# Layer 1 of a four-layer graph network on one Trainium2 core: its last eighth of sources in two pieces, one of them multiplied inside layer 0's last groups

## The chip, the core and the metric

The kernel runs on one core of one Trainium2 chip. The metric is the device time of one execution in microseconds (us); the kernel before has a median of 7455.67 us over 8 runs (7449.52 to 7474.21). The engines are named as the profile names them: PE (TensorE, with PEld for its weight loads), DVE (VectorE), ACT (ScalarE), POOL (GpSimd) and SP (SyncE, whose queue issues most DMAs here).

## What is computed

8192 nodes with 32 features, 262144 edges sorted by destination. Four message-passing layers, each followed by a residual sum and a layer norm over the 32 features:

```python
x = _layernorm(x + _L0_gnn_ref(x, L0_gnn_weight, src, dst, edge_type_64), axis=-1)
x = _layernorm(x + _L1_gnn_ref(x, edge_index, edge_weight), axis=-1)
x = _layernorm(x + _L2_gnn_ref(x, edge_index), axis=-1)
x = _layernorm(x + _L3_gnn_ref(x, edge_index, edge_attr_4, edge_attr_32, ...), axis=-1)
```

Layer 0 sums, at each destination, the source's row times one of 64 matrices. Layer 1 sums `x[src] * w` (w the edge's weight) and layer 2 sums `x[src]`. Layer 3 is an edge network and is not touched here.

## The kernel before, in words

The 8192 nodes stand as 64 blocks of 128 (a block's nodes on the 128 partitions). `LC = 8` blocks make a piece of 1024 nodes, and there are `NQ1 = 8` pieces.

**Layer 0** is a loop over 256 groups g of 1024 edges. For each group POOL gathers the eight sets of 128 rows by indirect DMA (L454), twelve groups ahead (`AHEAD`). The first four gathers of group g+12 wait for group g's own matmuls (`sums_of[g]`), the other four for what PE has been given by then (`now(PE)`). DVE builds one-hot rows (L583) and splits the gathered rows into three bf16 parts (L858 to L863). PE multiplies (eight matmuls, L897). Every fourth group DVE takes the sums out (`bank_out`, L869). As soon as all edges of a piece have passed, `windows` (L575) adds the shifted sums in PSUM and `normalize` (L525 to L537) writes the piece of `x_b`, layer 1's input. Piece k is known from group `ready(k)` on; the last piece, 7, only after group 255.

**Counts as dense matrices.** Groups 8 to 207 also make layer 1's weights and layer 2's counts as dense matrices: `matrices(i)`, 256 times, one-hot products on PE (L654), evicted by ACT (L658 for the counts, L659 for the weights into `st_a`) and stored by SP (L664 `famat`, L666 `fcmat`). A *square* `(c, z)` is the weights of 1024 sources (piece z) to 256 destinations (column c, 32 of them): 1 MB in `famat`, loaded by SP (L695) into a slot of 2048 words on each partition (`slot1`; three slots serve layer 0, three more the part behind it).

**Layer 1** is the sum over all 32 x 8 squares. `products(n, ...)` (L717) multiplies one square: 8 matmuls of a 128x32 block of `x_b` with 256 columns, four of them side by side in four column strips of the array (in the profile each fp32 matmul stands as two records, so a square is 16). The result, four strips by 256 columns, is taken to SBUF by ACT (`take`, L726), turned back and added over the strips by PE (`turn_back`, L736, two matmuls with `stack` as the moving operand), and added to `y1` by DVE (`add_up`, L752).

A planner written out by hand, `plan()`, decides which squares layer 0's groups multiply while their engines have time: `RATE` squares a group fall due (3.0 from group 200 on), a job is a run of pieces of one column, and at most two jobs end in one group, because bank 6 has two halves as accumulators (`bank[:, 6, 256*h:...]`) and `sums1` two. The order on PE within a group is: the group's eight L897 matmuls, `turn_back()` of the jobs that ended a group earlier, `matrices`, then `layer1(g)` with this group's squares. The squares wait for `acc_free`, which is the last `add_up` on DVE. Each square's slot is loaded again by `pump()` when PE has marked the square before it as used.

In this plan squares of piece 5 run in groups 198 to 218, squares of piece 6 (32 of them) in groups 230 to 245, two a group. From group 246 to 255 no group has a square. Piece 7 is normalized after group 255, and its 32 squares are left over (`late`).

**The tail** multiplies these 32 squares, one column a step: `products` (L717), `take` of 128x256 (L726), and, one step behind, `turn` (L980, two matmuls) into an output bank; every fourth step a whole piece is normalized for layer 2's input (with the three bf16 parts, L542 to L546). Six squares' loads are ahead of PE. Layer 2 (L1033) follows when the last piece is normalized.

Of the kernel before, what the change touches and what calls it, by code (L numbers as in the profile page):

```python
# [68 lines left out]

RATE = lambda g: 1.5 if g < 200 else 3.0  # L70


def plan():

    normed, n = [], 0
    for g in range(GG):
        if g >= 2 and (g - 2) % 4 == 3:
            while n < NQ1 and ready(n) <= g - 1:
# [24 lines left out]
    if job is not None:  # L103
        out[-1][4] = True
    return out
# [45 lines left out]
AW = 41200  # L151
NQ1 = 8
WIN = 48
# [8 lines left out]
def in_order(ctx: ExitStack, tc, x, a, w0, w1, b1, w2, si, keep):  # L162
# [11 lines left out]
    for k in range(2):  # L174
        m[f"amat{k}"] = dram.tile([NC1 // 2, NQ1, P * 2048 + 2304], FP, name=f"famat{k}")
    m["cmat"] = dram.tile([CB, P, 2048], U8, name="fcmat")
# [27 lines left out]
def raw_layers(tc, x, a, w0, w1, b1, w2, si, m, bad):  # L204
# [7 lines left out]
    ytab, xtab, hist, cmat = (m[k] for k in ("ytab", "xtab", "hist", "cmat"))  # L212
    amat = [m["amat0"], m["amat1"]]

# [42 lines left out]
    assert cut.at == 16384  # L257
    st_a = cut(2, 8, 4 * 64).rearrange("p b z (q h w) -> p b z q h w", q=4, h=2)
    st_c = cut(2, 4, 2, 256, dt=U8)
# [254 lines left out]

    lnf, lns = m["lnf"], m["lns"]
    x_st = Landing(tc, "st_x")
    ln_last = [None]

    def normalize(l, c, acc, pm, x_in, x_out, x3=None, more=None):


        ds = slice(c * LC, (c + 1) * LC)
        y, yc, sq = (lnf[:, k].rearrange("p (d f) -> p d f", f=D) for k in range(3))
        V.after(pm, ln_last[0])
# [4 lines left out]
        own(V, V.e.tensor_scalar(lns[:, 1], lns[:, 0], 1.0 / D, None, op0=OP.mult))  # L529
        vm = V.mark(V.e.tensor_sub(yc, y, lns[:, 1, :, None].to_broadcast([P, LC, D])))  # L530
        A.after(vm)
# [4 lines left out]
        xo = x_out[:, ds, :]  # L536
        ln_last[0] = V.mark(V.e.tensor_tensor(xo, yc, lns[:, 3, :, None].to_broadcast([P, LC, D]), op=OP.mult))  # L537
        if x3 is not None:
# [12 lines left out]

    def windows(c, acc, free):

        d0 = c * LC
        todo = []
        for j in [0, 1, 2, 3, -2, -1, 4]:
            lo, hi = 0, LC
# [73 lines left out]
    def matrices(i):  # L631
# [14 lines left out]
        for q in range(4):  # L646
# [4 lines left out]
            for j in range(4):  # L651
                for h in range(2):
# [11 lines left out]
        st_ld[b].add(S.e.dma_start(amat[i // 128][i // 8 % 16, :, 0:P * 2048].rearrange("z (p w) -> p z w", w=2048)[:, :, 256 * (i % 8):256 * (i % 8 + 1)],  # L664
                                   st_a[:, b].rearrange("p z q h w -> p z (q h w)")))
        stored[i] = st_ld[b].add(S.e.dma_start(cmat[i], st_c[:, b].rearrange("p u h c -> p (u h c)")))  # L666
# [6 lines left out]
    items = [(o[1], o[2]) for o in order1] + late  # L673
    m_ld = [Landing(tc, f"ld_m{k}") for k in range(8)]
    land1, used1, loaded = {}, {}, [0]
    acc_free = [None]
    sums1_free = [None, None]
    turned = []
    added = []
    normed = {}  # L680

    def slot_of(n):

        r = n - n_in
        if r < 0:
            return 3 + n % 3, n - 3
        order = [0, 1] + [3 + (n_in + k) % 3 for k in range(3)] + [2]
        return order[r % 6], n - 6 if r >= 6 else n - 5 if 2 <= r < 5 else None

    def load1(n, *more):  # L690

        c, z = items[n]
        k, before = slot_of(n)
        S.after(stored[8 * c + 6], stored[8 * c + 7], used1.get(before), *more)
        land1[n] = m_ld[k].add(S.e.dma_start(slot1[k], amat[c // 16][c % 16, z, 0:P * 2048].rearrange("(p w) -> p w", w=2048)))  # L695

    def pump():

        while loaded[0] < n_in + 5:
            n = loaded[0]  # L700
            c, z = items[n]
            before = slot_of(n)[1]
            if made < 8 * (c + 1) or (before is not None and before >= 0 and before not in used1):
                break
# [4 lines left out]
    def products(n, acc, first, last):  # L709

        c, z = items[n]
        k = slot_of(n)[0]
        PE.after(land1[n], normed[z])
        mv = slot1[k].rearrange("p (u h s j) -> p s u h j", h=2, s=8, j=4)
        for s in range(8):
            q = s % 4
            ins = PE.e.matmul(acc[q * D:(q + 1) * D, :].rearrange("p (u h j) -> p u h j", h=2, j=4),  # L717
                              x_b[:, 8 * z + s, :], mv[:, s], start=(first and s < 4), stop=(last and s >= 4),
                              tile_position=(0, q * D))
# [9 lines left out]
    def turn_back():  # L729
# [4 lines left out]
        for c, h, k, am in todo:  # L734
            for d in range(2):
                ins = PE.e.matmul(bank[:, 6, 256 * h + d * D:256 * h + (d + 1) * D], sums1[:, k, d * P:(d + 1) * P], stack,  # L736
                                  start=True, stop=True)
# [7 lines left out]
    def add_up():  # L745
# [3 lines left out]
        while added:  # L749
            c, h = added.pop(0)  # L750
            o, v = y1[:, 2 * c:2 * c + 2, :], bank[:, 6, 256 * h:256 * h + 2 * D].rearrange("p (d f) -> p d f", f=D)
            acc_free[0] = own(V, V.e.tensor_copy(o, v) if c not in begun1 else V.e.tensor_add(o, v, o))  # L752
            begun1.add(c)
# [3 lines left out]
    def layer1(g):  # L757

        ended = []
        while order1 and order1[0][0] == g:  # L760
            _, c, z, first, last, h = order1.pop(0)
            n = n_in - len(order1) - 1
            PE.after(acc_free[0])
            pm = products(n, bank[:, 6, 256 * h:256 * (h + 1)], first, last)
            pump()
            if last:
                ended.append((c, h))
        for c, h in ended:
            turned.append((c, h, h, take(sums1[:, h], bank[:, 6, 256 * h:256 * (h + 1)], pm, sums1_free[h])))
        pump()  # L770
# [34 lines left out]
    def early_counts(g):  # L805

        k = g - soon[0]
        if k == 0:
            ring_free[0] = ring_free[1] = now(PE)
            for n in (n_in, n_in + 1):  # L810
                load1(n, stored[CB - 2], stored[CB - 1])
# [118 lines left out]
    for c in range(NC1):  # L930
        if c not in begun1:
            V.e.memset(y1[:, 2 * c:2 * c + 2, :], 0.0)
    while loaded[0] < min(len(items), n_in + 6):
        load1(loaded[0], *end)
# [37 lines left out]
    def turn(l, c, n, am):  # L972

        nb = 2 if l == 1 else 4
        kk = 128 if l == 1 else 96
# [7 lines left out]
        if d0 + nb == LC:  # L983
            out_free[o] = normalize(l, c * nb // LC, bank[:, 2 + o, 0:LC * D], pm, x_b if l == 1 else x_a,
                                    x_a if l == 1 else x_b, x3 if l == 1 else None,
# [6 lines left out]
    n = n_in  # L992
    for c in range(NC1):
        b = c % 2
        PE.after(sum_bank[b])
        for e in range(got[c], NQ1):
            pm = products(n, bank[:, b, 0:256], e == got[c], e == NQ1 - 1)
            if n + 6 < len(items):
                load1(n + 6)
            n += 1  # L1000
        sum_bank[b] = am = take(sums[:, b, 0:256], bank[:, b, 0:256], pm, sum_free[b])
        if pend:
            turn(*pend)
        pend = (1, c, c, am)
        if c == 0:
            widen(0, [2])
# [193 lines left out]
    for q in range(NQ + LAG3 + 2):  # L1200
# [73 lines left out]
        if 0 <= c < NQ and c % 2 == 1:  # L1274
# [9 lines left out]
            while done < NB // LC and ready(done) <= g + 1:  # L1284
                k, wp = w_bank()
                acc = bank[:, 3 + 2 * k, 0:LC * D]
                windows(done, acc, (w_free[k], gm))
                w_free[k] = normalize(3, done, acc, PE.mark(written(3 + 2 * k, 256)), z, x_a)
                done += 1
# [471 lines left out]
```

## Time and profile before

| | |
|---|---|
| median of 8 runs | 7455.67 us |
| the profiled execution's own time | 7456.69 us |
| its span | 7455.0 us |
| PE busy | 5089.0 us (68%) |
| DVE busy | 4413.7 us (59%) |
| POOL busy | 4141.1 us (56%) |
| ACT busy | 2252.3 us (30%) |
| layer 0's last eight matmuls (L897, group 255) start | 4002.56 us |
| first product of the tail (L717) | 4013.60 us |
| first matmul of layer 2 (L1033) | 4110.82 us |

Times are counted from the span's start. A line of the timeline is: start, duration, engine, line of the kernel, operation, what it writes and reads, shape, how many records are merged in it, and in brackets how long the engine had been idle and what ended that ("remote" when the profile finds no releaser). A line of the windows view gives the length of a stretch, each engine's busy time with its number of instructions, the granted TensorE clock, the DMA engines' share and GB/s. Starts of matmuls are recorded; their ends are modelled, so what tells when PE had really finished is the start of the instruction that waited for it.

### The profile page before, as it was taken

To read this page: it belongs to the slowest core of one execution; us is meant where nothing else is said; L and a number is where in the kernel's file an instruction comes from. 1 tells how busy PE (TensorE), PEld (TensorE's weight loads), DVE (VectorE), ACT (ScalarE), POOL (GpSimd) and SP (SyncE) were. 2 spreads that over 40 slices of the span, in tenths; PEclk is the share of its full clock that TensorE was granted. 3 is DMA by queue.
4 is the path that set the end of the run, shared out by engine and by line. 5 is a ranking of instruction groups with operands and counts; after the bars stand their busy time and mean duration, and the time that the engine had idled before them with its cause. 6 is when DMAs were issued, how large, how long until landed. Compare 5 with 4: busy or idle time off the path is not lost.

```text
span 7455.0 us, 89563 instructions
## 1 busy us (share of the span) xinstructions
PE 5089.0 (68%) x34750; PEld 3360.6 (45%) x34750; DVE 4413.7 (59%) x9506; ACT 2252.3 (30%) x3323; POOL 4141.1 (56%) x4236
## 2 busy tenths in 40 slices
PE   7236566656666666667337977787878787877777
PEld 3125555555555555555224534444444444444444
DVE  3246566566565565555324647666666676676666
ACT  5223333333333333333101832222222222222222
POOL 3655555454454444444661666666666666666664
PEclk7556776777777777777555989888989888888889
DMA  9324444545655656667536731111111111111111
GB/s 352 92 56 142 132 144 141 171 143 165 207 163 188 207 182 205 215 216 247 183 119 229 274 92 25 24 25 21 25 24 24 25 24 25 24 25 24 24 24 18
DMA packets 583331, 865.52 MB, mean 116 GB/s; under 512 B 102640, under 2 KB 441840, under 8 KB 549360
## 3 DMA queue, kind: packets, MB, share of 16 engines
q1 hardware_dynamic: 448320, 782.88, 30.3%
q0 software_dynamic: 134144, 73.67, 6.5%
q8 instruction: 276, 4.52, 0.3%
q10 hardware_dynamic: 432, 3.15, 0.1%
q14 instruction: 159, 1.30, 0.1%
HBM read 454.48 MB, written 404.88 MB: 115 GB/s over the span
## 4 chain that ended last, share of the span: by engine, by line
PE 37%; another core or an unknown queue 25%; DVE 20%; ACT 9%; issue 7%; DMA 2%; POOL 1%; SPq 0%; DVEq 0%; ACTq 0%; POOLq 0%
PE bank L654 14%; PE bank L1221 7%; DVE f_arena L1256 4%; PE bank L1211 4%; ACT f_arena L659 3%; ACT f_arena L658 3%; PE bank L1033 3%; DVE f_arena L1252 3%; PE bank L717 2%; DVE f_arena L588 2%; DVE f_arena L1249 2%; DVE f_arena L1240 1%; ACT bank L1190 1%; PE bank L475 1%
## 5 line engine op out<-in xcount | busy, mean ns | idle before, releaser
L454 POOL DMA_INDIRECT f_arena<-fytab,f_row x2048 | 1961.6, 958 | 1795.6 <-PE bank L654 745.9
L454 POOL DMA_INDIRECT f_arena<-fxtab,f_src x2048 | 1942.2, 948 | 1108.7 <-issue 564.9
L654 PE MATMUL bank<-f_arena 64*128 64x128 f32 x16384 | 1517.7, 353 | 933.9 <-ACT f_arena L659 522.1
L654 PEld LDWEIGHTS bank<-f_arena 64*128 64x128 f32 x16384 | 1385.3, 257 | 1042.2 <-issue 549.0
L1221 PE MATMUL bank<-f_arena 128*128 128x344 f32 x4096 | 1484.8, 506 | 54.6 <-issue 54.4
L658 ACT ACTIVATE f_arena<-bank 128x512 uint8<-128x512 f32 x1024 | 612.8, 598 | 1787.2 <-remote 859.3
L1221 PEld LDWEIGHTS bank<-f_arena 128*128 128x128 f32 x4096 | 815.9, 210 | 630.8 <-issue 368.0
L1211 PE MATMUL bank<-f_arena 64*128 64x256 f32 x4096 | 662.9, 447 | 549.6 <-ACT bank L1190 436.9
L1190 ACT ACTIVATE bank<-f_arena 128x1024 f32<-128x1024 f32 x512 | 526.2, 1029 | 1141.9 <-DVE f_arena L1256 681.0
L1211 PEld LDWEIGHTS bank<-f_arena 64*128 64x128 f32 x4096 | 393.2, 207 | 940.6 <-ACT bank L1190 563.2
L1249 DVE TENSOR_TENSOR f_arena<-bank,f_arena 128x256 f32<-128x256 f32 x512 | 214.0, 418 | 872.5 <-remote 536.2
L638 DVE TENSOR_TENSOR f_arena<-bank,f_arena 128x1024 f32<-128x1024 bf16 x256 | 312.8, 1222 | 647.0 <-PE bank L654 423.3
L659 ACT ACTIVATE f_arena<-bank 128x512 f32<-128x512 f32 x1024 | 611.0, 597 | 0.0
L640 DVE TENSOR_TENSOR f_arena<-bank,f_arena 128x2048 f32<-128x2048 bf16 x256 | 586.6, 2291 | 8.8
L1256 DVE TENSOR_TENSOR f_arena<-bank,f_arena 128x256 f32<-128x256 f32 x1536 | 550.3, 413 | 0.0
L1177 ACT ACTIVATE f_arena<-bank,f_arena 128x512 f32<-128x512 f32 x256 | 175.7, 686 | 1122.8 <-remote 649.9
L717 PE MATMUL bank<-f_arena,f_x_b 128*32 128x256 f32 x4096 | 394.5, 525 | 63.5 <-DMA f_arena<-famat 21.2
L897 PE MATMUL bank<-f_arena 128*128 128x96 bf16 x2048 | 181.3, 238 | 260.5 <-DVE f_arena L863 135.1
L588 DVE TENSOR_TENSOR f_arena<-bank,f_rel 128x512 f32<-128x512 f32 x512 | 348.3, 680 | 0.0
L1252 DVE TENSOR_TENSOR f_arena<-bank,f_arena 128x512 f32<-128x512 f32 x512 | 348.2, 680 | 0.0
L643 DVE TENSOR_TENSOR f_arena<-f_arena,bank 128x1024 f32<-128x1024 f32 x256 | 309.6, 1209 | 0.0
L752 DVE TENSOR_TENSOR f_arena<-bank,f_arena 128x64 f32<-128x64 f32 x127 | 28.5, 224 | 470.2 <-PE bank L736 364.8
(149 smaller groups left out, 4651.1 us busy)
## 6 DMA issues: line engine op xcount, KB each, us to landing
famat<-f_arena SPq DMA_DIRECT2D x256, 1024.0 KB
f_arena<-famat SPq DMA_DIRECT2D x256, 1024.0 KB, 5.3
fytab<-f_arena SPq DMA_DIRECT2D x64, 1024.0 KB
fcmat<-f_arena SPq DMA_DIRECT2D x256, 256.0 KB
f_arena<-fcmat SPq DMA_DIRECT2D x16, 4096.0 KB, 14.8
f_arena<-fytab,f_row POOLq DMA_INDIRECT x2048
f_arena<-fxtab,f_src POOLq DMA_INDIRECT x2048
f_arena<-laid_ea SPq DMA_DIRECT2D x64, 512.0 KB
```

The costliest lines, as they stand in the source:

```text
L454: return G.e.indirect_dma_start(out=dest, out_offset=None, in_=table, in_offset=bass.IndirectOffsetOnAxis(ap=ix, axis=0))
L588: return V.e.tensor_tensor(o, iota[:, None, :].to_broadcast([P, n, P]), rel[:, t:t + n, None].to_broadcast([P, n, P]), op=OP.is_equal)
L640: V.e.tensor_tensor(oh_l[:, b], iota2[:, None, :, 0].to_broadcast([P, 16, P]), meta_l[:, pp, k0:k0 + 16, None].to_broadcast([P, 16, P]), o ...
L654: ins = PE.e.matmul(two[:, h].rearrange("p (c s j) -> p c s j", s=64, j=4)[:, :, :, j], oh_l[hs_, b, 4 * q + j, :], oh_k[hs_, b, 4 * q + j ...
L658: A.e.activation(st_c[:, b, q], two[:, :, 0:256], AF.Copy)
L659: pair_free[u] = am = A.mark(A.e.activation(st_a[:, b, :, q].rearrange("p z h w -> p h z w"), two[:, :, 256:512].rearrange("p h (z w) -> p ...
L717: ins = PE.e.matmul(acc[q * D:(q + 1) * D, :].rearrange("p (u h j) -> p u h j", h=2, j=4), x_b[:, 8 * z + s, :], mv[:, s], start=(first an ...
L1190: return A.mark(A.e.activation(wp, b2_s[:, None, :].to_broadcast([P, 4, 256]), AF.Copy))
L1211: ins = PE.e.matmul(wp[:, t, :], hs[hp, q // 2 % 2, c0:c0 + P], w2_s[hp], start=False, stop=True, skip_group_check=True)
L1221: ins = PE.e.matmul(bank[:, g % 2, 0:MW], oh[:, c % NO, t, :], p[:, c % NP, t, :], start=(c % 2 == 0 and t == 0), stop=(c % 2 == 1 and t = ...
L1252: V.e.tensor_tensor(pq[:, :, 0:128].rearrange("p t (o k) -> p t o k", k=16), wp[:, :, 0:128].rearrange("p t (o k) -> p t o k", k=16), a0[: ...
L1256: ins = V.e.tensor_tensor(pq[:, :, 128 + 64 * mm:192 + 64 * mm].rearrange("p t (o i) -> p t o i", i=8), wp[:, :, 192:256].rearrange("p t ( ...
```

## The change

The pieces are written down as a list `SEG`: seven of 8 blocks, and two of 4 blocks (blocks 56 to 59 and 60 to 63). `NQ1` becomes 9. `known(z)` takes the place of `ready` for layer 0: piece 7 (4 blocks) is known at group 241 and normalized at group 245; piece 8 is normalized after group 255.

- The weights of the last eighth get an array of their own, `flast`, 32 columns x 2 pieces of 512 KB; `matrices` stores each matrix's share in it with one more DMA (256 more in all), and ACT's eviction writes runs of 16 words where it wrote 32.
- Half a slot (1024 words) is now the unit: twelve halves, of which six are layer 0's ring; a full square takes two, a half square one. The order of the words within a square changes with it, and so does the access pattern of the moving operand.
- From group 210 on up to four jobs may end in a group (`ROOMS`); the accumulators 2 and 3 are the halves of bank 2, which `matrices` no longer needs then, and `sum1` has four.
- The plan that comes out: groups up to 209 as before; piece 5 ends in group 216 (groups 210, 213, 214 and 215 have three squares where they had two); piece 6 takes groups 230 to 240 with three squares each (the last two); groups 246 to 253 have the 32 half squares of piece 7, four each, four jobs each.
- The tail has 32 half squares (512 sources, four matmuls each). Two columns share a bank and make one step: `take` is 128x512, `turn` has four matmuls, and there are 16 steps. Twelve half loads are ahead of PE.
- `windows` and `normalize` work on a piece of any number of blocks.

```diff
+SEG = [(8 * k, 8) for k in range(7)] + [(56, 4), (60, 4)]
+NQ1 = len(SEG)
+ROOMS = lambda g: 4 if g >= 210 else 2
+def known(z):
+    return min(GG, 4 * (sum(SEG[z]) - 1) + 5)
...
-                room = NQ1 if ended == 0 else int(due) if ended == 1 else 0
+                room = 0 if ended == ROOMS(g) else NQ1 if ended == 0 else int(due)
...
-            due -= 1
+            due -= SEG[z][1] / 8
...
+    m["last"] = dram.tile([NC1, 2, P * 1024 + 2304], FP, name="flast")
...
-                two[:, :, 256:512].rearrange("p h (z w) -> p h z w", w=32), AF.Copy))
+                two[:, :, 256:512].rearrange("p h (z w) -> p h z w", w=16), AF.Copy))
...
+        st_ld[b].add(S.e.dma_start(last8[i // 8, :, 0:P * 1024].rearrange("z (p w) -> p z w", w=1024)[:, :, P * (i % 8):P * (i % 8 + 1)],
+                                   st_a[:, b, 14:16].rearrange("p z q h w -> p z (q h w)")))
...
-        mv = slot1[k].rearrange("p (u h s j) -> p s u h j", h=2, s=8, j=4)
-        for s in range(8):
+        s0, ns = SEG[z]
+        mv = place(k, w).rearrange("p (i f v s j) -> p f s i v j", i=8, f=w, v=8, j=4)
+        for s in range(ns):
...
-            PE.after(acc_free[0])
-            pm = products(n, bank[:, 6, 256 * h:256 * (h + 1)], first, last)
+            PE.after(acc_free[0], *(pair_free if h >= 2 else ()))
+            pm = products(n, acc1[h], first, last)
...
-            while done < NB // LC and ready(done) <= g - 1:
-                acc = bank[:, (g - 2) // per % 2, 0:LC * D]
-                agg_free[(g - 2) // per % 2] = vm = normalize(0, done, acc, windows(done, acc, (vm,)), x_a, x_b)
+            while done < NQ1 and known(done) <= g - 1:
+                d0, nd = SEG[done]
+                acc = bank[:, (g - 2) // per % 2, 0:nd * D]
+                agg_free[(g - 2) // per % 2] = vm = normalize(0, d0, acc, windows(d0, acc, (vm,)), x_a, x_b)
...
-    for c in range(NC1):
-        b = c % 2
+    for c2 in range(NC1 // 2):
+        b = c2 % 2
         PE.after(sum_bank[b])
-        for e in range(got[c], NQ1):
-            pm = products(n, bank[:, b, 0:256], e == got[c], e == NQ1 - 1)
-            if n + 6 < len(items):
-                load1(n + 6)
-            n += 1
-        sum_bank[b] = am = take(sums[:, b, 0:256], bank[:, b, 0:256], pm, sum_free[b])
+        for c in (2 * c2, 2 * c2 + 1):
+            for e in range(got[c], NQ1):
+                pm = products(n, bank[:, b, 256 * (c % 2):256 * (c % 2 + 1)], e == got[c], e == NQ1 - 1)
+                if n + 12 < len(items):
+                    load1(n + 12)
+                n += 1
+        sum_bank[b] = am = take(sums[:, b], bank[:, b], pm, sum_free[b])
```

More of the change, by code (lines that the diff above doesn't have):

```diff
@@ L77, in plan @@
         if g >= 2 and (g - 2) % 4 == 3:
-            while n < NQ1 and ready(n) <= g - 1:
+            while n < NQ1 and known(n) <= g - 1:
                 n += 1
@@ L512, in gathers, with normalize @@
         return k, under_way[-(WT // TP):]
-    lnf, lns = m["lnf"], m["lns"]
+    lnf = m["lnf"]
     x_st = Landing(tc, "st_x")
     ln_last = [None]
-    def normalize(l, c, acc, pm, x_in, x_out, x3=None, more=None):
-        ds = slice(c * LC, (c + 1) * LC)
-        y, yc, sq = (lnf[:, k].rearrange("p (d f) -> p d f", f=D) for k in range(3))
+    def normalize(l, d0, acc, pm, x_in, x_out, x3=None, more=None):
+        nd = acc.shape[-1] // D
+        ds = slice(d0, d0 + nd)
+        y, yc, sq = (lnf[:, k, 0:nd * D].rearrange("p (d f) -> p d f", f=D) for k in range(3))
+        lns = m["lns"][:, :, 0:nd]
         V.after(pm, ln_last[0])
@@ L550, in normalize, with windows @@
         return read
-    def windows(c, acc, free):
-        d0 = c * LC
+    def windows(d0, acc, free):
+        nd = acc.shape[-1] // D
         todo = []
         for j in [0, 1, 2, 3, -2, -1, 4]:
-            lo, hi = 0, LC
+            lo, hi = 0, nd
             while 4 * (d0 + lo) + j < 0:
@@ L673, in raw_layers @@
     items = [(o[1], o[2]) for o in order1] + late
-    m_ld = [Landing(tc, f"ld_m{k}") for k in range(8)]
+    assert all(z >= 7 for _, z in late)
+    m_ld = [Landing(tc, f"ld_m{k}") for k in range(12)]
+    home, at, user = [], 0, {}
+    for n in range(n_in):
+        k = SEG[items[n][1]][1] // 4
+        at += at % k
+        home.append((6 + at % 6, k, [user.get(6 + (at + e) % 6) for e in range(k)]))
+        for e in range(k):
+            user[6 + (at + e) % 6] = n
+        at += k
+    turns = [0, 1, 2, 3] + [6 + (at + e) % 6 for e in range(6)] + [4, 5]
+    for n in range(n_in, len(items)):
+        k = turns[(n - n_in) % 12]
+        home.append((k, 1, [user.get(k)]))
+        user[k] = n
     land1, used1, loaded = {}, {}, [0]
     acc_free = [None]
-    sums1_free = [None, None]
+    sums1_free = [None] * 4
+    acc1 = [bank[:, 6 - 4 * (k // 2), 256 * (k % 2):256 * (k % 2 + 1)] for k in range(4)]
+    sum1 = [sums1[:, 0], sums1[:, 1]] + [late_slot[2][:, 256 * k:256 * (k + 1)] for k in range(2)]
     turned = []
@@ L680, in raw_layers, with place @@
     normed = {}
[L682 to L688, printed above, removed]
+    def place(k, w):
+        return slot1[k // 2][:, 1024 * (k % 2):1024 * (k % 2 + w)]
     def load1(n, *more):
         c, z = items[n]
-        k, before = slot_of(n)
-        S.after(stored[8 * c + 6], stored[8 * c + 7], used1.get(before), *more)
-        land1[n] = m_ld[k].add(S.e.dma_start(slot1[k], amat[c // 16][c % 16, z, 0:P * 2048].rearrange("(p w) -> p w", w=2048)))
+        k, w, before = home[n]
+        S.after(stored[8 * c + 6], stored[8 * c + 7], *(used1.get(b) for b in before), *more)
+        from_ = amat[c // 16][c % 16, z] if w == 2 else last8[c, z - 7]
+        land1[n] = m_ld[k].add(S.e.dma_start(place(k, w), from_[0:P * 1024 * w].rearrange("(p w) -> p w", w=1024 * w)))
     def pump():
-        while loaded[0] < n_in + 5:
+        while loaded[0] < n_in + 10:
             n = loaded[0]
             c, z = items[n]
-            before = slot_of(n)[1]
-            if made < 8 * (c + 1) or (before is not None and before >= 0 and before not in used1):
+            if made < 8 * (c + 1) or any(b is not None and b not in used1 for b in home[n][2]):
                 break
@@ L711, in products @@
         c, z = items[n]
[L712 removed]
+        k, w, _ = home[n]
+        s0, ns = SEG[z]
         PE.after(land1[n], normed[z])
[L714 to L715 removed]
+        mv = place(k, w).rearrange("p (i f v s j) -> p f s i v j", i=8, f=w, v=8, j=4)
+        for s in range(ns):
             q = s % 4
[L717 to L718 removed]
+            ins = PE.e.matmul(acc[q * D:(q + 1) * D, :].rearrange("p (i v j) -> p i v j", v=8, j=4),
+                              x_b[:, s0 + s, :], mv[:, s // 4, q], start=(first and s < 4), stop=(last and s >= ns - 4),
                               tile_position=(0, q * D))
@@ L768, in layer1 @@
         for c, h in ended:
-            turned.append((c, h, h, take(sums1[:, h], bank[:, 6, 256 * h:256 * (h + 1)], pm, sums1_free[h])))
+            more = (stored[CB - 1], stored[CB - 2]) if h >= 2 else ()
+            turned.append((c, h, h, take(sum1[h], acc1[h], pm, sums1_free[h], *more)))
         pump()
@@ L809, in early_counts @@
             ring_free[0] = ring_free[1] = now(PE)
-            for n in (n_in, n_in + 1):
+            for n in range(n_in, n_in + 4):
                 load1(n, stored[CB - 2], stored[CB - 1])
@@ L972, in turn @@
     def turn(l, c, n, am):
-        nb = 2 if l == 1 else 4
+        nb = 4
         kk = 128 if l == 1 else 96
@@ L983, in turn @@
         if d0 + nb == LC:
-            out_free[o] = normalize(l, c * nb // LC, bank[:, 2 + o, 0:LC * D], pm, x_b if l == 1 else x_a,
+            out_free[o] = normalize(l, c * nb // LC * LC, bank[:, 2 + o, 0:LC * D], pm, x_b if l == 1 else x_a,
                                     x_a if l == 1 else x_b, x3 if l == 1 else None,
```

27 lines of the change are left out of this document (13 added, 14 removed).

## The prediction

> **What bounds it now.** I read the page, then the windows of the stages, then the timeline around layer 0's end and the tail. The change moves nothing before group 210; behind the tail everything only follows. So three stretches count: groups 210 to 245, groups 246 to 255, the tail.
>
> ```profile
> core 0: us, PE busy (x) PEld busy (x) DVE busy (x) ACT busy (x) POOL busy (x), PEclk, DMA share, GB/s
> 3810.00:3960.00 150.00, 77.43 (x618) 46.14 (x617) 45.64 (x120) 8.32 (x24) 96.50 (x103) 0.61 0.59 196
> 3973.00:4003.00 30.00, 8.22 (x86) 6.42 (x84) 27.25 (x67) 0.00 (x0) 0.00 (x0) 0.54 0.15 63
> 4013.00:4103.00 90.00, 89.40 (x633) 47.16 (x633) 34.80 (x95) 19.97 (x46) 2.94 (x1) 0.50 0.84 316
> ```
>
> The first row (groups 232 to 244) shows no engine full; the second (246 to 255) is DVE's, with PE free; the third, the tail, is PE's alone, at half clock.
>
> A group with two squares, while gathers run:
>
> ```profile
> 3822.53 3.64 PE L717 MATMUL bank<-f_arena,f_x_b 128*32 128x256 f32 x32 [0.57 <-DVE f_arena L752]
> ...
> 3828.33 0.95 POOL L454 DMA_INDIRECT f_arena<-fytab,f_row  x1 [0.30 <-issue]
> 3830.98 0.69 ACT L726 ACTIVATE f_arena<-bank 128x256 f32<-128x256 f32 x2 [11.05 <-remote]
> 3831.31 0.94 POOL L454 DMA_INDIRECT f_arena<-fytab,f_row  x1 [2.04 <-remote]
> ...
> 3831.82 1.89 PE L736 MATMUL bank<-f_stack,f_arena 128*128 128x32 f32 x8 [4.89 <-ACT f_arena L726]
> ...
> 3833.74 0.48 DVE L752 TENSOR_TENSOR f_arena<-bank,f_arena 128x64 f32<-128x64 f32 x2 [7.71 <-PE bank L736]
> ```
>
> Two squares stand there with 3.64 us, but `take`, which waits for nothing else, starts 8.45 us after they began, and so does POOL, which waits for the L897 behind them. The modelled end (3826.17) is wrong by 4.8 us. The round is 8.45 + 0.84 (to L736) + 1.9 + 0.5 + gaps = 11.75 us, and POOL, whose own need is 8 x 1.25 = 10.0, pauses 2.0 of it. Without gathers the same two squares end as modelled:
>
> ```profile
> 3963.33 3.64 PE L717 MATMUL bank<-f_arena,f_x_b 128*32 128x256 f32 x32 [0.57 <-DVE f_arena L752]
> ...
> 3967.04 0.69 ACT L726 ACTIVATE f_arena<-bank 128x256 f32<-128x256 f32 x2 [6.31 <-PE bank L717]
> ...
> 3967.88 1.27 PE L736 MATMUL bank<-f_stack,f_arena 128*128 128x32 f32 x8 [0.15 <-ACT f_arena L726]
> ...
> 3969.72 1.93 PE L717 MATMUL bank<-f_arena,f_x_b 128*32 128x256 f32 x32 [0.57 <-DVE f_arena L752]
> ```
>
> PE is at half clock at 3963 and at full clock at 3969 (3.64 against 1.93 us for the same work). A step of the tail:
>
> ```profile
> 4032.46 1.94 PE L717 MATMUL bank<-f_arena,f_x_b 128*32 128x256 f32 x16
> ...
> 4034.33 1.06 PE L980 MATMUL bank<-f_stack,f_arena 128*128 128x32 f32 x4
> 4034.47 0.41 ACT L726 ACTIVATE f_arena<-bank 128x256 f32<-128x256 f32 x1 [2.44 <-PE bank L717]
> ...
> 4035.32 1.94 PE L717 MATMUL bank<-f_arena,f_x_b 128*32 128x256 f32 x16
> ```
>
> No idle time stands in PE's rows: a column costs 2.86 us, of it 0.96 the turn.
>
> **The change part by part** (sums against the profiled execution, 7456.7 us; the median shown is 1.0 less).
>
> *The tail.* A new step has 16 product records (as one column now: 1.90 us) and eight turn records. L736 spaces them 0.215 us, so the turn is 0.96 + 4 x 0.215 = 1.82; step 3.73, sixteen steps. Now 4013.6 to 4102.9 is 89.3 us; then 15 x 3.73 + 1.9 less the first step's missing turn (1.8) = 56. A wider last take and turn give back 1.6. **Gain 31 us.** What hides beside it: normalizing costs DVE 5.84 us (4038.29 to 4044.13) each two steps of 3.73, so it fits; loads fall from 26 MB in 89 us to 10 MB in 56. If DVE did not fit, its 5.84 would only replace 3.73 x 2 from 7.5 on.
>
> *Piece 8 after group 255.* From L897's end (4003.38) to the first product (4013.60) is 10.2 us, of it 6.0 for 28 shift matmuls (L575). Four blocks need 18: 3.9; the half-wide DVE operations save about 0.7. 7.4 us, **gain 2.8**, counted below.
>
> *Groups with three squares* (210, 213 to 215, and 231 to 239; 230 is a case by itself). No steady row shows them. Bounds: in group 211 three squares of one column began at 3581.23, and POOL's next gather came 11.88 us after the one before: 11.9 at the least, with one take and one turn where the new ones have three. At the most every square costs half of 8.45: 12.7 + takes 1.0 + turns 2.75 + adds 0.75 + gaps 0.3 = 17.4. Between: PE is late while POOL gathers, and POOL's gathers end 9.7 us after it starts, 4.3 of them before the products; 5.4 us at 4.2 a square leave 1.7 squares at 1.71 = 2.9, and 1.0 to 2 us lag (two squares show 1.0 more than this reckoning), so 4.3 + 5.4 + 2.9 + 1.4 = **14.0 us**; I take it, as group 211's burst (9.1 us from the first product at 3581.23 to PE's semaphore at 3590.31) gives 9.1 + 4.8 = 13.9 too. Groups 210 to 215: 4 x 2.25 = 9 more, groups 217 and 218 without squares give POOL back 2 x 1.75: **+5.5**. Then 3807.5 (the first squares' take now) + 5.5 + 2 (third square) + 9 x 14.0 + 11.75 (group 240, two) puts the end of piece 6's squares at 3952.8, against 3971.7 now. POOL has three groups of gathers (30 us) left there.
>
> *Groups 241 to 253.* From 3952.8: 7 us of turns, adds and parts, three groups at 2.97, at 245 the sums, 14 shift matmuls (3.0 us) and normalizing (about 3), then 246: its products start after 26.6 and, partly under gathers, end after 33.2. A group of four half squares then goes round as the 3963 row does: products 3.64, takes 0.69 + 2 x 0.3, turns (16 records, 3.6 at half clock, 1.9 at full) 2.7, adds 4 x 0.25, gaps 0.3: **8.9 us** where a group costs 2.97 now. Products of 253 start after 33.2 + 5.3 + 6 x 8.9 = 92, its turns and adds end after 101, group 255 after 105, the tail starts after 112: at 4064.8. Bounds: all at full clock 6.6 a round, all at half 9.9.
>
> *Rest.* 256 more store issues on SP (0.37 to 0.59 us each) stand before loads; SP waits 1876 us for L659 in the matrices' time, so nothing, at most 6 us through the 17 waits for a load. L659 with runs of 16 words: `take` writes single words at 0.41 us, as L532 writes a row (0.42), so nothing. The products' denser stride shows in no row: nothing, bounds 5 us either way. Loads of 32 half squares go from the tail to groups 246 to 253; two of a group's four are ahead, the others have 8.9 us against 5.3 for 1 MB.
>
> **Sum:** tail start 4013.6 to 4064.8 is +51.2, tail -31: **+20, 7476 us**. What is late next is ACT and PE's round inside the group, which takes the place of a dense tail: a half square costs 2.2 us in a group and 1.4 (2.86 / 2) in the old tail.
>
> [...]
>
> **Rivals.**
> (A) *The third square rides free.* Group 211 speaks for it: three squares released 9.1 us after their start against 8.45 for two. At 11.9 us a group 13 x 2.1 = 27 less: 7449, faster than before. It decides from 12.6 us a group (20 / 13 below 14.0). With full clock in groups 246 to 253 also (7 x 2.3): 7433. Against it: three takes and turns, not one.
> (B) *Every square is late by the same 4.2 us*, as 231 to 243 show one after another: 17.4 us, 13 x 3.4 = +44: 7520.
> (C) *The change doesn't do what it says*: the tail stays at some other bound, DVE or loads, and the 31 us don't come: 7507.
>
> **How the numbers follow.** Forecast (7457 to 7497) 0.48; A 0.27, of it 0.15 below 7441; B 0.18; C 0.05; 0.02 elsewhere. About 0.2% (15 us) is what a measurement of this kernel can tell from no change: below 7441 0.15; 7441 to 7471 0.28; above 0.57. The range goes from A's end with full clock, 7438, to 7515, short of B.
>
> **What would show it.** Right: steps of 3.7 us in the tail, 16 of them; POOL's rounds of about 14 us in groups 231 to 239; rounds near 9 us in 246 to 253; layer 2 some 20 us after 4110.8. Wrong: rounds of 12 or 17 us; rounds of 6.6; a tail at full clock; a change before group 210.

## The result, and the profile after

The changed kernel takes **7488.6 us** (median of 13; 7469.4 to 7498.1) against 7458.0 us of the kernel before in the same runs (36 of them): ratio **1.0041, 95% interval 1.0033 to 1.0049**, so 31 us slower. Forecast were 7476 us and slower. The profiled execution took 7493.0 us, its span is 7491.3.

Starts of single stages in the two profiled executions, in us. "Groups" are the starts of L897 (before) and L923 (after); the tail is from its first product to layer 2's first (L1033, L1060).

| | before | after | difference |
|---|---|---|---|
| group 210 | 3566.1 | 3595.6 | +29.5 |
| group 246 | 3972.8 | 4001.4 | +28.6 |
| group 255 | 4002.6 | 4078.8 | +76.2 |
| tail's first product | 4013.6 | 4087.2 | +73.6 |
| layer 2 | 4110.8 | 4147.1 | +36.3 |
| end of the span | 7455.0 | 7491.3 | +36.3 |

So three things happened: 29.5 us were lost before group 210, where the forecast had nothing; 47.6 in groups 246 to 255; and the tail gave 37.3 back (97.2 to 59.9 us). From group 210 to group 246 the two are alike (406.7 and 405.8 us). The stages' windows of the changed kernel, which answer to those of before:

```profile
core 0: us, PE busy (x) PEld busy (x) DVE busy (x) ACT busy (x) POOL busy (x), PEclk, DMA share, GB/s
3845.00:3955.00 110.00, 77.40 (x612) 45.05 (x604) 34.04 (x93) 8.80 (x27) 70.08 (x75) 0.62 0.74 265
4001.00:4079.00 78.00, 59.33 (x460) 39.78 (x461) 35.00 (x99) 10.12 (x32) 0.00 (x0) 0.57 0.63 216
4087.00:4144.00 57.00, 50.75 (x384) 33.01 (x384) 36.57 (x100) 17.68 (x32) 4.40 (x2) 0.62 0.63 237
```

The second row is the one to look at: before, groups 246 to 255 took 30 us, set by DVE alone (busy 27.25 of a window of 30.00, PE 8.22); now they take 78, PE works 59 of them, and POOL still does nothing: its gathers are all done. A round of these groups in the changed kernel's timeline:

```profile
4023.61 3.59 PE L760 MATMUL bank<-f_stack,f_arena 128*128 128x32 f32 x16 [0.72 <-ACT f_arena L750]
4027.24 1.00 DVE L776 TENSOR_TENSOR f_arena<-bank,f_arena 128x64 f32<-128x64 f32 x4 [5.24 <-PE bank L760]
4028.30 3.64 PE L741 MATMUL bank<-f_arena,f_x_b 128*32 128x256 f32 x32 [1.09 <-DVE f_arena L776]
...
4032.01 1.26 ACT L750 ACTIVATE f_arena<-bank 128x256 f32<-128x256 f32 x4 [8.54 <-PE bank L741]
...
4033.41 3.59 PE L760 MATMUL bank<-f_stack,f_arena 128*128 128x32 f32 x16 [0.72 <-ACT f_arena L750]
```

Turn, add, product, take, turn: each waits for the one ahead of it, and the round is 33.41 - 23.61 = 9.8 us. A group with three squares, while gathers run:

```profile
3879.07 5.11 PE L741 MATMUL bank<-f_arena,f_x_b 128*32 128x256 f32 x48 [0.83 <-DVE f_arena L776]
...
3886.89 0.98 ACT L750 ACTIVATE f_arena<-bank 128x256 f32<-128x256 f32 x3 [10.91 <-PE bank L923]
3888.01 2.74 PE L760 MATMUL bank<-f_stack,f_arena 128*128 128x32 f32 x12 [1.12 <-ACT f_arena L750]
3890.79 0.74 DVE L776 TENSOR_TENSOR f_arena<-bank,f_arena 128x64 f32<-128x64 f32 x3 [8.69 <-PE bank L760]
...
3891.59 5.35 PE L741 MATMUL bank<-f_arena,f_x_b 128*32 128x256 f32 x48 [0.83 <-DVE f_arena L776]
```

12.5 us here, and 11.9 in the mean of groups 233 to 239. And two steps of the tail:

```profile
4098.50 1.08 PE L1006 MATMUL bank<-f_stack,f_arena 128*128 128x32 f32 x8 [0.86 <-ACT f_arena L750]
4099.51 1.07 PE L741 MATMUL bank<-f_arena,f_x_b 128*32 128x256 f32 x16
...
4104.44 1.08 PE L1006 MATMUL bank<-f_stack,f_arena 128*128 128x32 f32 x8 [1.85 <-ACT f_arena L750]
4105.45 1.92 PE L741 MATMUL bank<-f_arena,f_x_b 128*32 128x256 f32 x16
...
4109.15 1.94 PE L741 MATMUL bank<-f_arena,f_x_b 128*32 128x256 f32 x16
```

The step from 4105.45 to 4109.15 is 3.70 us, as forecast (3.73). From 4098.50 to 4104.44 PE is at full clock (1.07 us for the same 16 products), and two steps take 5.94 us, held up by the normalizing: from 4100.62 to 4106.45 DVE and ACT have 5.83 us of it in this timeline, and the turn at 4104.44 waits 1.85 us for ACT's `take`, which stands behind it.

### The profile page after: what moved, and what is told of

It is laid out like the page before. It is cut to its first block, busy times and chain, and to the rows that moved or that the text cites. A ratio compares the mean times of both kernels' runs of the same rounds, so it can differ in the third digit from the quotient of the medians.

```text
span 7491.3 us, 90184 instructions
## 1 busy us (share of the span) xinstructions
PE 5086.0 (68%) x34884; PEld 3368.9 (45%) x34884; DVE 4421.9 (59%) x9545; ACT 2258.7 (30%) x3341; POOL 4141.6 (55%) x4236
## 4 chain that ended last, share of the span: by engine, by line
PE 36%; another core or an unknown queue 24%; DVE 20%; ACT 9%; issue 8%; DMA 2%; POOL 1%; SPq 0%; DVEq 0%; ACTq 0%; POOLq 0%
PE bank L664 15%; PE bank L1248 6%; DVE f_arena L1283 4%; PE bank L1238 4%; PE bank L1060 3%; ACT f_arena L669 3%; ACT f_arena L668 3%; DVE f_arena L1279 3%; PE bank L741 3%; DVE f_arena L598 2%; DVE f_arena L1276 2%; PE bank L483 1%; DVE f_arena L1267 1%; PE bank L760 1%
## 5 line engine op out<-in xcount | busy, mean ns | idle before, releaser
L668 ACT ACTIVATE f_arena<-bank 128x512 uint8<-128x512 f32 x1024 | 612.7, 598 | 1809.7 <-remote 930.1
L923 PE MATMUL bank<-f_arena 128*128 128x96 bf16 x2048 | 181.4, 239 | 318.0 <-DVE f_arena L888 218.1
L923 PEld LDWEIGHTS bank<-f_arena 128*128 128x128 bf16 x2048 | 125.1, 114 | 421.5 <-DVE f_arena L888 230.3
```

The source lines that it names most:

```text
L668: A.e.activation(st_c[:, b, q], two[:, :, 0:256], AF.Copy)
```

## The experiments

**Theory 1:** the price is the half squares of groups 246 to 253, which ride free only if something else holds these groups up, plus the second store of every matrix (+29.5 by group 210). **Rivals:** the word order of the stored weights (runs of 16) costs the first part; the first part is scatter of single executions; the third square pays; the pairs alone pay.

*A thing to know first.* The kernel before itself came in two conditions. In the runs of the result and beside the last experiment it takes 7439 to 7458 us; in the three sets between, 5775 to 5786 us. All kernels of a set share the condition, so ratios are read within a set. I call them **late** (7.4 ms) and **prompt** (5.8 ms), for this: in the late profile of before, `take` (L726) starts 2.06 us (median of 91) after the modelled end of the products when POOL is issuing gathers and 0.07 us (median of 26, 24 of them in the tail) when it isn't; in the prompt profile with the word order changed both are 0.07 us (75 and 24 takes). Counted are takes before which ACT was idle, "issuing" means a gather within 2 us. The second and the fourth set carry the same chip number on record, so the condition does not go with that number.

The same wait of the changed kernel in both, the normalizing of a block (L535) behind 18 shift matmuls (L585), first late, then prompt:

```profile
3743.28 5.51 PE L585 MATMUL bank<-f_arena,f_shift 128*128 128x256 f32 x18 [4.52 <-issue]
3809.19 0.42 DVE L535 TENSOR_TENSOR f_lnf<-bank,x_a 128x256 f32<-128x256 f32 x1 [65.97 <-remote]
```

```profile
2555.40 4.66 PE L585 MATMUL bank<-f_arena,f_shift 128*128 128x256 f32 x18
2560.10 0.42 DVE L535 TENSOR_TENSOR f_lnf<-bank,x_a 128x256 f32<-128x256 f32 x1 [4.91 <-PE bank L585]
```

60 us against none. In the late one POOL issues 64 gathers without a pause up to 3805.24, until its ring of twelve groups is full (the next, at 3816.79, waits 11.55 us for L923); DVE is let go 4 us after that, at 3809.19. So late executions have the gathers 10 groups ahead at group 246, and there the groups without squares cost 3.0 to 3.4 us each. Prompt ones have them one to three groups ahead from group 228 on, one at group 246: there a group costs 10.0 us in the mean, POOL's 8 x 1.25, with squares or without.

**Set 1, prompt (before: 5774.8 us, 28 runs).** The parts alone, and the change with one store.

*One more store.* Before, with

```
-        st_ld[b].add(S.e.dma_start(amat[...][i // 8 % 16, :, ...], st_a[:, b]))
+        for zs in (slice(0, 7), slice(7, 8)):
+            st_ld[b].add(S.e.dma_start(amat[...][i // 8 % 16, zs, ...], st_a[:, b, zs]))
```

> The kernel before with one edit: each matrix's weights are stored by two DMAs (seven pieces, and the eighth by itself), same rows of 1 KB, same places. In the profile of the change group 210 starts 29.5 us later than before (3595.6 against 3566.1), where I had forecast no change. Theory 1: the second store of each matrix costs that, by its issue on SP and by its descriptors; then this kernel is 15 to 30 us slower than before and group 210 starts at about 3590. Theory 2: the order of the words costs it (eviction in runs of 16, denser stride of the products); then this kernel is within 5 us of before. Theory 3: it is the scatter of single executions (the runs of before lie between 7441 and 7478); then within 5 us here and in all the others.

5775.4 us, ratio 1.0001 (0.9992 to 1.0010): no difference at the end, where 15 to 30 us were expected from the second store. But its profile reaches group 210 at 2451.5 us, and those of the other three of this set, with one store, at 2432.0 to 2440.0. The wait of L658 for a store to land, with one store (the kernel below) and with two:

```profile
  DMA fcmat<-f_arena: 118.9, 37
```

```profile
  DMA fcmat<-f_arena: 142.8, 40
```

Over all prompt profiles with all gathers: 127.5 to 142.8 us with a second store, 99.4 to 118.9 without. The same line's wait for PE is shorter in exchange (709.7 to 715.9 us against 719.4 to 740.8), so that all its waits together differ less, 849 to 857 us against 835 to 848: the later start of group 210 goes with the second store, but that this one wait makes it is argued and not shown.

*Word order.* Before, with the change's runs of 16 words and its strides:

```
-    st_a = cut(2, 8, 4 * 64)
+    st_a = cut(2, 16, 128)
-        mv = slot1[k].rearrange("p (u h s j) -> p s u h j", h=2, s=8, j=4)
+        mv = slot1[k].rearrange("p (i f v s j) -> p f s i v j", i=8, f=2, v=8, j=4)
```

> The kernel before with one edit: the words of a square in the order of the change (eviction L659 in runs of 16 words, the products' moving operand with a stride of 16 words where it was 32), stored by one DMA as before. Theory 1 (second store): within 5 us of before. Theory 2 (order of the words): 25 to 30 us slower, group 210 at about 3595, and L659 or L717 longer than 592 and 633 ns. Theory 3 (scatter): within 5 us.

5773.5 us, 0.9998 (0.9989 to 1.0007): nothing.

*The change with one store.* All nine pieces in one array, the halves read as 512-byte rows:

```
-        st_ld[b].add(... amat, st_a[:, b, 0:14] ...); st_ld[b].add(... last8, st_a[:, b, 14:16] ...)
+        st_ld[b].add(S.e.dma_start(amat[...], st_a[:, b].rearrange("p (z f) q h w -> p z (f q h w)", f=2)))
```

> The changed kernel with one edit: one store DMA for each matrix, rows of 1 KB in which the two halves of the last eighth stand side by side; a half square is then read in rows of 512 B where the change reads rows of 4 KB. Theory 1 (second store): 7455 to 7462 us, group 210 near 3566. Theory 2 (order of the words): 7485 to 7490. Theory 3 (scatter): 7488 in the median like the change. The 512 B rows could cost in groups 246 to 253 and in the tail, if loads there become late: then the loss is seen in waits of the products for famat.

5755.2 us, **0.9967 (0.9955 to 0.9979)**: faster than before by 20 us, the other sign than the change had in the late runs. (The times expected above were those of late runs.)

*Three squares a group.* Before, with a third accumulator:

```
+ROOMS = lambda g: 3 if g >= 210 else 2
-                room = NQ1 if ended == 0 else int(due) if ended == 1 else 0
+                room = 0 if ended == ROOMS(g) else NQ1 if ended == 0 else int(due)
```

> The kernel before with one edit: from group 210 on three jobs may end in a group (accumulator 2 in bank 2, a third sum), so piece 5 ends in group 216 and piece 6 in group 240; piece 7 stays whole, in the tail. My prediction put a group of three at 14.0 us; the changed kernel's profile shows POOL rounds of 12.0. Theory 1: a third square rides along (rounds of 12.0), and groups 241 to 255 are held up until POOL has issued its last gather and then need DVE's 3 us each: 0 to 8 us faster than before. Rival: groups 241 to 255 keep close behind POOL: 25 to 30 us faster. Rival as predicted: rounds of 14 us, 10 to 25 us slower.

5775.2 us, 1.0003 (0.9994 to 1.0012): nothing.

**Set 2, prompt (before: 5777.1 us, 22 runs).** The change itself, the pairs alone, the change without its half squares.

> The changed kernel itself, beside three others on one chip. Theory 1: its price lies in groups 246 to 253 and depends on how many groups the gathers are ahead of the products there. Where they are 10 groups ahead (the first profiles), a group without squares takes 2.97 us and four half squares make it 8 to 9.8: slower by about 30 us. Where they are one group ahead (the four kernels above, 10.0 us a group with or without squares), the half squares cost nothing, and the tail's 30 us are left: ratio 0.995 to 0.997. Theory 2 (the second store of every matrix, or the flast array, costs time): slower than the kernel with one store by 0.1 to 0.5% in either place.

The change: 5757.9 us, **0.9967 (0.9955 to 0.9979)**, as with one store. The second store costs nothing here in the end. The same 60 us, groups 248 to 253, in the kernel with only the word order changed and in the change:

```profile
2740.00:2800.00 60.00, 4.93 (x48) 3.66 (x48) 18.23 (x43) 0.00 (x0) 45.37 (x49) 0.50 0.08 14
```

```profile
2740.00:2800.00 60.00, 45.53 (x362) 30.95 (x354) 24.64 (x69) 8.85 (x28) 45.31 (x49) 0.59 0.71 242
```

Columns as in the windows above: PE goes from 4.9 to 45.5 us, and POOL issues the same 49 gathers in the same time. The half squares are hidden, and the shorter tail is the gain: 64.3 us against 96.0 in these two profiles. How much that is depends on the clock granted to the long tail: at 0.51 it takes 96.0 us, at 0.75 and above 82 to 83 (last section); 19 us, the difference of the medians, is nearer to the second.

*Pairs alone.* Before, with the tail's columns turned by two:

```
-        nb = 2 if l == 1 else 4
+        nb = 4
-    for c in range(NC1):
+    for c2 in range(NC1 // 2):
+        for c in (2 * c2, 2 * c2 + 1):
```

> The kernel before with its tail in pairs alone: 32 whole squares, two destination columns in one bank, one take and eight turn records a step. The groups are those of before. By the tail's rows (2.86 us a column, of it 0.96 the turn) a pair would take 2 x 1.90 + 1.82 = 5.6 us against 5.7: nothing to gain, ratio 0.999 to 1.001, if the pairs are worth nothing by themselves. If the turns' start-up is what pairs save (rival), 16 x 0.5 to 1 us: 8 to 16 us faster, 0.997 to 0.9985.

5778.9 us, 1.0004 (0.9994 to 1.0013): nothing to gain.

*The change without half squares in groups 246 to 253* (they are done in the tail):

```
-RATE = lambda g: 1.5 if g < 200 else 3.0
+RATE = lambda g: 1.5 if g < 200 else 3.0 if g < 246 else -9.0
```

> The changed kernel without the half squares of groups 246 to 253: all 64 half squares are left to the tail. Theory 1: where the gathers are 10 groups ahead, groups 246 to 255 take some 33 us again and not 86, and the tail is 30 us longer: about 20 us faster than the change. Where they are one ahead, the groups take 10 us all the same and the tail is 30 us longer: slower than the change by 30 us, so equal to before within 0.1%. If the half squares cost nothing anywhere (rival), it is 30 us slower than the change in both places.

5776.9 us, 0.9999 (0.9990 to 1.0008), as expected: all of the change's 19 us are gone. The half squares under the gathers are the whole gain.

**Set 3, prompt, but with the gathers out of the way (before, with all gathers: 5785.7 us, 9 runs).** In all four kernels of this set three of four gathers of groups 200 to 255 are left out, so that POOL is far ahead as in the late profiles (10 groups at group 246), while nothing is late (`take` starts 0.07 us after its products in all four):

```
+            if table is not ytab or s * WT + t < 8 * 200 or t % 4 == 0:
                 indirect(xg[:, k, t, :], table[:, :], ix[...]).then_inc(ld.sem, 16)
```

> The kernel before with three of four gathers of groups 200 to 255 left out (the rows of an earlier gather stand in their place, so the sums of those groups are of wrong rows): POOL then needs 2.5 us a group there and not 10, and is as far ahead of the products as in the first profiles. Reference for the three kernels beside it. Theory 1: groups 246 to 255 go at 2.97 us and not at 10.0, and the groups with two squares at 6.6: some 60 to 100 us less than before, ratio 0.983 to 0.990.

> The kernel before with every matrix's weights stored by two DMAs, and the same gathers left out (three of four in groups 200 to 255). Theory 1: the profiles with a second store reach group 210 at 2451 to 2455 us, those without at 2432 to 2443, and lose it again behind gathers that hold the groups up anyway. Without these it stays: 10 to 15 us slower than the reference beside it. Rival (the offset at group 210 is scatter of single executions): no difference.

> The changed kernel without the half squares of groups 246 to 253, and the same gathers left out (three of four in groups 200 to 255). Theory 1: groups 246 to 255 take 33 us again, the tail 83 us and not 64: faster than the changed kernel beside it by 20 to 30 us, and within 10 us of the reference. Rival: slower than the changed kernel by 19 us, as with all gathers.

> The changed kernel with the same gathers left out (three of four in groups 200 to 255). Theory 1 (the half squares ride free only where the gathers hold the groups up): groups 246 to 253 take 8 to 9.8 us with four half squares and not 2.97, +45; the second store's 12 to 15 us are no longer swallowed by the gathers; the tail still gives 30: slower than the kernel before with the same gathers left out by 15 to 35 us (0.3 to 0.6%). Rival (the first profiles' loss is of that chip alone, from PE's late completions): faster by 19 us as on this chip with all gathers.

| kernel, few gathers | median, us | range | of before | 95% interval |
|---|---|---|---|---|
| before | 5649.1 | 5634.5 to 5661.1 | 0.9773 | 0.9756 to 0.9790 |
| + second store | 5660.4 | 5652.7 to 5670.3 | 0.9796 | 0.9782 to 0.9809 |
| + third square, pairs (no half squares in groups) | 5683.8 | 5681.5 to 5689.9 | 0.9830 | 0.9817 to 0.9844 |
| + half squares: the change | 5708.0 | 5696.8 to 5729.6 | 0.9864 | 0.9847 to 0.9882 |

The sign turns: with nothing to hide under, the change is **59 us slower** than before (5708.0 - 5649.1). That is more than the 15 to 35 us expected, and the first line gained more than expected too (137 us, not 60 to 100). Each line costs. The second store: 11 us by medians (the two intervals overlap; at group 210 of the profiles 15, as expected). The half squares: 24 us, as expected (20 to 30). With all gathers the same half squares gained 19 us (5776.9 - 5757.9): the same edit, with the sign turned by the gathers alone. The stages of the kernel without half squares in the groups, and of the change; rows are groups 230 to 240, 246 to 254, and the tail:

```profile
2569.00:2670.00 101.00, 74.65 (x717) 42.86 (x710) 39.55 (x108) 9.85 (x31) 20.74 (x22) 0.71 0.85 317
2694.00:2722.00 28.00, 7.40 (x72) 5.50 (x72) 27.04 (x66) 0.00 (x0) 0.00 (x0) 0.50 0.00 1
2730.00:2813.00 83.00, 66.32 (x640) 35.32 (x640) 40.03 (x107) 21.24 (x34) 4.41 (x2) 0.75 0.96 373
```

```profile
2585.00:2690.00 105.00, 76.83 (x722) 43.17 (x721) 40.09 (x110) 9.96 (x31) 20.74 (x22) 0.68 0.84 307
2715.00:2787.00 72.00, 53.37 (x456) 34.52 (x456) 34.62 (x98) 10.10 (x32) 0.00 (x0) 0.64 0.68 234
2796.00:2859.00 63.00, 56.63 (x384) 36.38 (x376) 37.92 (x104) 20.32 (x34) 3.98 (x2) 0.53 0.63 231
```

28 us become 72, and 83 become 64: 44 paid for 19 to 20.

The third line I had not expected (within 10 us of the first, I wrote; it is 35 above, 11 of that the store). By the profiles groups 230 to 246 take 101.6 us with two squares a group and the second store, and 126.3 with three. Two squares go round in 6.5 us, three in 9.25 (groups 230 to 240: 101.8 / 11): 3.1 to 3.25 a square either way, so nothing is saved in them, and the five groups without squares (241 to 245) still take 24.5 us, 9.9 of them group 244, behind which piece 7 is normalized. The two profiles also differ by 15.7 us ahead of group 230, which no run explains.

**Set 4, late (before: 7439.3 us, 11 runs).** The change with one store and two squares a group up to 245; only half squares and pairs are left of it.

```
-ROOMS = lambda g: 4 if g >= 210 else 2
+ROOMS = lambda g: 4 if g >= 246 else 2
```

> The changed kernel with one store for each matrix (as in the kernel with one store above) and at most two squares a group until group 245, as before; the half squares of groups 246 to 253 and the tail in pairs stay. Theory 1: the third square saves nothing (three squares take 9.25 us where gathers don't hold a group up, two 6.3), and the second store costs 11 us that gathers swallow. Where gathers hold the groups up from 228 on, this one is as fast as the change, 0.9955 to 0.998 of the kernel before; where they are far ahead (an execution like the first profiles), it loses only the half squares' 44 us against the tail's 37: within 0.2% of before, and 20 us or more faster than the change. Rival: the third square is what makes room for the half squares; then it is slower than the change by 10 us or more in either place.

7478.8 us, 1.0045 (1.0031 to 1.0059): **my expectation fell**. It is neither within 0.2% of before nor faster than the change (1.0041). Its profile against that of before: group 210 at 3566.0 (before 3566.1), group 246 at 3988.8 (+16.0), group 255 at 4068.1 (+65.5), tail 60.2 against 97.2, layer 2 +25.9. So the 29.5 us ahead of group 210 do go with the second store, and with them longer waits ahead of L658, 1808 us in all against 1785 here and 1786 in before. Most of the difference stands in its "remote" row, for which the profile finds no releaser (before 859.3), first the change, then this kernel:

```profile
  remote: 930.1, 203
```

```profile
  remote: 820.2, 183
```

but 16.0 us are lost again by group 246: group 228 lasts 62.4 us here, 25.5 in before, 77.8 in the change. In the change this is the stall that lasts until POOL's ring is full (above). From group 210 to group 246 this kernel takes 422.8 us, the change 405.8 and before 406.7, so in these single profiles the third square seems to gain something. The two ratios' intervals overlap, so the rival (the third square makes the room for the half squares) is not settled. What remains, the half squares' 49.5 us (groups 246 to 255) for the tail's 37, is seen in both late profiles.

No version beats the others in both conditions: in prompt runs the change and its form with one store lead (0.9967); in late runs the kernel before does.

## Why the prediction was right, point by point

- **The side was right, and so was its mechanism:** a dense tail was traded for a round in the group which nothing covers. The runs with few gathers show it by taking the half squares out and putting them in.
- **The size was near (+20 forecast, +31 by medians, +36 by profiles), but by luck.** Of the profiles' 36.3 us, 29.5 arose before group 210, where the forecast had nothing. From there on the tail's start moved by 44.1 us (51.2 forecast) and the tail gave 37.3 (31 forecast): 6.8 us where the sum had 20. Two of the signs of being wrong that the prediction named came true, rounds of 12 us and a change before group 210. Nor is the store simply the missing term: the late kernel with one store, and two squares a group, was 0.45% slower than before all the same.
- **One bound doesn't agree with itself:** the range's lower end, 7438, is called rival A's end with full clock, which the rivals put at 7433. The result lies far from both.
- **The tail: 31 forecast, 37 measured**, with a clock of 0.62 granted and not the 0.50 I worked with. At 0.53, in the prompt profile of the change, the tail takes 64.3 us, 31.7 less than one whole tail at 0.51 (96.0): the step's sum holds at the clock it was made for.
- **Groups 246 to 255:** forecast to go from 29.8 to about 79 us; 77.4 measured. Rounds are 7.9 to 9.8 us where I wrote 8.9, at a granted clock of 0.57 in the mean.
- **Piece 8:** 7.4 us forecast from L897's end to the first product; 7.6 measured.
- **Three squares: 14.0 us forecast, 11.9 measured.** Rival A had this number, but not its consequence: the 27 us it promised did not come. The stalls at groups 228 and 244 (77.8 and 27.7 us; before 25.5 and 12.0) took more than that (groups 230 and 231 gave 30.8 back, 26.9 after 57.7), and group 246 starts 28.6 us later, hardly less than group 210. Under late gathers the third square itself is almost free (11.9 us a group, 11.7 with two); where no gathers hold the group up it costs 2.8 us (9.25 and 6.5), and nothing is saved.
- **"256 more store issues ... so nothing, at most 6 us" is the step that failed.** I priced SP's issue time and the loads behind it. The measured term is +29.5 us at group 210 (late) and 11 to 15 (prompt). With it goes, in prompt profiles, a longer wait of ACT for stores to land before it may write the staging buffer again (L658: 127.5 to 142.8 us against 99.4 to 118.9), and in the late one of the change a longer wait at the same line that the profile gives to nobody (930.1 us against 859.3). By which way the store costs the time stays open.
- **A condition I did not see:** the forecast took it as given that the gathers are all done by group 246. Where they hold the groups up, the same change gains 0.33%. Row "POOL 0.00" of groups 246 to 255 was the thing that decided the sign.

What stays open: why the instructions that wait for PE start late while POOL issues gathers in some sets of runs (2.06 us) and not in others (0.07); why the second store lengthens that wait; and what takes back, by group 246, half of what one store gains in late runs. Kernels that would separate these were not run, nor was the change without its half squares in the late condition.

## What to carry over

Work moved into a group is free only while something else holds that group up, so ask which engine ends the group's round and whether it will still do so; here it was POOL's 10 us in one condition and only DVE's 3 us in the other, and the same change gained 19 us or lost 31. Packing more of a serial chain (product, take, turn, add) into one round bought nothing here where only the chain set the round (3.1 to 3.25 us a square, with two or three), each link waited for the last and the emptied rounds kept their own cost (24.5 us for five). Do not price an added store by its issue alone (priced here at nothing, measured at 11 us with few gathers): look also at what waits for it to land.

## What was not expected of the hardware

The kernel before took 5775 to 5786 us in some sets of runs and 7439 to 7458 in others, at mean granted clocks of 0.868 to 0.878 and 0.788 to 0.797. The clock isn't the whole of it: in the late profile, handing products from PE to ACT took 2.06 us (median) while gathers were being issued and 0.07 us otherwise, and in the changed kernel one handing over to DVE took 60 us longer late than prompt.

The tail with all of the last eighth in it can go at either clock. The windows of two prompt tails with the same 640 matmuls, first two columns a step, then one:

```profile
2822.00:2905.00 83.00, 61.22 (x640) 34.88 (x640) 40.26 (x108) 21.77 (x34) 4.42 (x2) 0.79 0.93 377
```

```profile
2817.00:2913.00 96.00, 90.10 (x640) 48.62 (x640) 38.89 (x107) 23.70 (x50) 4.40 (x2) 0.51 0.83 319
```

At the clock of 0.79 PE needs 61 us and not 90, but the tail is only 13 us shorter: the DMA engines are then at 0.93 and not 0.83, and PE has no matmul for 21.8 us of its stretch (83.00 - 61.22), where it was 5.9 (96.00 - 90.10). It isn't the pairs: with few gathers the tail of before went at 0.82 too, in 81.6 us, and the products that start there at 2722.15 and 2724.64 had waited 0.57 and 0.36 us for loads of `famat`. So what a shorter tail gains goes with the clock of the long one: 96.0 us at 0.51, 81.6 at 0.82. Being busy does not go with the higher clock here: the tail that is busy for 90.1 of 96 us has 0.51, and the one busy for 61.2 of 83 has 0.79. What decides which of the two a tail gets, no run shows.
